# Four heads scored together in the last unit, the last batch leaving in two parts, moved fills and a reordered expert choice in a one-core attention kernel

## The chip, the cores and the metric

The kernel runs on one NeuronCore of a Trainium2 chip. A core has five engines with queues of their own: TensorE (PE; its weight loads are listed apart as PEld), VectorE (DVE), ScalarE (ACT), GpSimd (POOL), and SyncE (SP), which here only issues DMA transfers. TensorE multiplies a stationary operand with a moving one and writes to PSUM, eight banks of 512 floats per partition; the other engines bring results from there to SBUF. Each engine works its own queue in order and waits on semaphores for the others. The metric is device time in microseconds (us), as the median of several runs.

## The reference

The input is 8 sequences of 1024 tokens of 256 floats. Three residual steps follow one another:

```python
x = x + 0.5 * ffn(layernorm(x), ...)      # mixture of 8 experts, top 2, capacity 1280
x = x + attention(layernorm(x), ...)      # 16 heads of 16, causal
x = x + 0.5 * ffn(layernorm(x), ...)
```

In `ffn` each token chooses two of 8 experts by a softmax gate. An expert is kept only if at most 1280 of the 16384 choices name it:

```python
counts = jnp.bincount(a_e, length=E)
keep = counts <= cap
```

An expert that is over capacity contributes nothing. Attention is ordinary: projections to q, k, v, scores with a causal mask, softmax, values, an output projection with bias.

## The kernel before

The kernel bets that no expert is kept. It runs attention on `x` directly, computes the gate of both expert layers beside it and counts the choices; at the end one flag decides whether the expert layers must be run at all (`tc.If(flag(either, "either") > 0)`). With the inputs used here the branch is not taken, so the time is that of `attention` and the flag.

**Units.** `attention` (L663) works in 32 units: 8 batches of 4 groups, each of 4 heads. A head's 16 dimensions take a stripe of 32 partitions, so a group fills 128. For a unit u two series of 24 steps exist. `m_steps(u + 1)` computes the next unit's scores once for their row maxima (tiles `sm`; VectorE reduces them into `first` and `top`). `e_steps(u)` computes this unit's scores again, transposed and with the maximum subtracted (tiles `sc`, 128 keys by up to 512 queries); ScalarE takes the exponential into `pT`, POOL zeroes the masked part of blocks on the diagonal (`affine_select`), and TensorE multiplies with the values (`pav`). A unit has two halves `hf` of 512 queries, with 4 and 8 blocks `jb` of 128 keys; a step k is one pair `pr` of heads of one block. The step loop issues the two scores of one pair, each followed by one of the next unit's maxima: four matmuls on four stripes of rows. Value products are owed for two or three steps and then issued in two parts. In the last unit (u = 31) there is no next unit, and a step has only its own two scores.

**PSUM.** Six single-bank buffers rotate over all score tiles (`score`), and two (`bank`) over everything else: value sums, projections, transposes.

**Order.** While attention runs, `InOrder` (L27) keeps each compute engine's instructions in the order of the program text. Its line, L37, therefore stands for nearly all instructions in the profile. `Beside` (L52) mixes side work into the steps: a generator yields a number of steps to wait, or `PIECE`, and a call of `step` then runs one piece. `settle` (L871) transposes the maxima and makes `qE`, the query with its maximum; `project` (L801) makes q and k of two groups and sends each head's rows to its stripe by DMA (`kT`, `qT`); `values_of` makes the values.

**Leaving.** The value sums of a group are copied to SBUF (`att`) and stored to DRAM (`att_d`). After the fourth group of a batch, `leave(b, hf)` (L954) loads all 16 heads and their softmax sums back in another layout (`on`, `sums`), inverts the sums, sends them through DRAM to spread them (`inv_d`, `inv`), multiplies on POOL, and projects (`px`, eight 32-column matmuls per block of 128 tokens), adding to the residual `xa`. `ln_stats` and `regate` (L1004) then give the second gate's logits, `choose` (L327) picks two experts per token and the tally is updated. For the last batch the first half's leave starts in step 9 of the last unit, and the second half's runs after all units:

```python
            drain(leave(B - 1, 1))
            drain(regate(B - 1, HT, TB))
```

**Choice.** `choose` subtracts the maximum logit, takes the exponential on ScalarE, normalises, and finds the largest key and then the second largest, each as a one-hot tile.

**End.** `any_kept` (L389) sums a tally over partitions with a matmul by ones, compares with the capacity and reduces to one number per layer; both numbers are combined, cast to an integer and read by all engines.

**Opening.** Weights are loaded on ScalarE's and SP's queues, transposed, and copied. VectorE first scales `bqT`, then takes the statistics of the first batch, then reduces `row16` to `one16`, a column with 1 in each stripe's 17th row. ScalarE copies `one16` into `kT` of four units (two before the first weight copy). Both halves of the first two groups are projected (L1072); of each, SP sends kT, and ScalarE's queue sends the first group's qT.

The pool tag `packed` has four buffers, used by the weights at first and by the projections after them.

Of the kernel before, what the change touches and what calls it, by code (L numbers as in the profile page):

```python
# [10 lines left out]
F32 = mybir.dt.float32  # L11
I32 = mybir.dt.int32
# [6 lines left out]
P = 128  # L19
# [81 lines left out]
def macaron_kernel(  # L101
# [59 lines left out]
    def mm(name):  # L161
# [13 lines left out]
    iota_e = const.tile([P, E], F32, name="iota_e")  # L175
    gpsimd.iota(iota_e, pattern=[[1, E]], base=0, channel_multiplier=0, allow_small_or_imprecise_dtypes=True)

    row16 = const.tile([P, 4], F32, name="row16")
    gpsimd.memset(row16, 0.0)
    gpsimd.affine_select(  # L180
        out=row16, in_=row16, pattern=[[-32, 4]], compare_op=ALU.not_equal, fill=1.0, base=-HD, channel_multiplier=1
    )
    one16 = const.tile([P, 1], F32, name="one16")
    vector.tensor_reduce(one16, row16, AX.X, ALU.max)

    tops = []
    for k in range(2):
# [20 lines left out]
    def weights(pool, bank, matmul, transpose):  # L208
# [16 lines left out]
            nc.sync.dma_start(out=boT, in_=bo.rearrange("(c p) -> p c", p=P))  # L225
            nc.sync.dma_start(out=bvT, in_=bkv[D:].rearrange("(c p) -> p c", p=P))

        vector.tensor_scalar(bqT, bqT, QSCALE, None, ALU.mult)

        def turn(wsb, dst):  # L230
            pt = bank("pt_w")
# [95 lines left out]
    def choose(rp, tag, n, lg):  # L327
        def new(name, shape=(P, n, E), dt=F32):
            return rp.tile(list(shape), dt, tag=f"{name}{n}", name=f"{name}_{tag}")

        def over_e(a):
            return a.unsqueeze(2).to_broadcast([P, n, E])

        mx = new("mx", (P, n))
        vector.tensor_reduce(mx, lg, AX.X, ALU.max)
        lc = new("lc")
        vector.tensor_tensor(lc, lg, over_e(mx), ALU.subtract)
        prob = new("prob")
        scalar.activation(prob, lc, AF.Exp)
        yield 1  # L340
        sm = new("sm", (P, n))
        vector.tensor_reduce(sm, prob, AX.X, ALU.add)
        vector.reciprocal(sm, sm)
        vector.tensor_tensor(prob, prob, over_e(sm), ALU.mult)
        yield 1

        key = new("key")
        vector.tensor_scalar(key, prob, TINY, 1.0, ALU.is_ge, ALU.subtract)
        vector.scalar_tensor_tensor(key, key, 1e30, lc, ALU.mult, ALU.min)
        yield 1  # L350
        ohs = []
        for k in range(2):
            best = new("best", (P, n))
            vector.tensor_reduce(best, key, AX.X, ALU.max)
            cand = new("cand")
            vector.tensor_tensor(cand, key, over_e(best), ALU.is_equal)
            yield 1

            vector.scalar_tensor_tensor(
                cand, cand, -100.0, iota_e.unsqueeze(1).to_broadcast([P, n, E]), ALU.mult, ALU.add  # L360
            )
            first = new("first", (P, n))
            vector.tensor_reduce(first, cand, AX.X, ALU.min)
            yield 1
            oh = new(f"oh{k}")
            vector.tensor_tensor(oh, cand, over_e(first), ALU.is_equal)
            if k == 0:
                vector.scalar_tensor_tensor(key, oh, -1e32, key, ALU.mult, ALU.add)
            ohs.append(oh)
            yield 1  # L370
        both = new("both")
        vector.tensor_tensor(both, ohs[0], ohs[1], ALU.add)
        return prob, ohs, both

    def run(steps):
        while True:
# [9 lines left out]
        return tally  # L386


    def any_kept(layer, tally, ps):  # L389
        nc.tensor.matmul(  # L390
            ps[:, : TB * E], lhsT=ones, rhs=tally.rearrange("p t e -> p (t e)"), start=True, stop=True
        )
        counts = route.tile([P, E], F32, tag="counts", name=f"counts{layer}")
        vector.tensor_reduce(counts, ps[:, : TB * E].rearrange("p (t e) -> p e t", e=E), AX.X, ALU.add)
        vector.tensor_scalar(counts, counts, float(CAP), None, ALU.is_le)
        some = route.tile([P, 1], F32, tag=f"some{layer}", name=f"some{layer}")
        vector.tensor_reduce(some, counts, AX.X, ALU.max)
        return some

    def flag(some, what):  # L400
        word = route.tile([P, 1], I32, tag="word", name=f"word_{what}")
        vector.tensor_copy(word, some)
        return nc.values_load(word[0:1, 0:1], min_val=0, max_val=1)


    def routing(layer, logits, wts, slots, idx):
        with tc.tile_pool(name=f"rt{layer}", bufs=1) as rp:
# [4 lines left out]
            def over_t(a):  # L412
                return a.unsqueeze(1).to_broadcast([P, NT, E])

            prob, ohs, both = run(choose(rp, f"r{layer}", NT, logits))

            before = new("before", (P, P))
            make_upper_triangular(nc, before, val=1.0, diag=False)
# [244 lines left out]
    def attention(run_no, src, dst, gate0, logits, tally):  # L663
# [3 lines left out]
        with stack:  # L667
# [125 lines left out]
            def gate_first(b):  # L793
                if gate0 is not None:
                    lg = gate0[0][:, b * TB : (b + 1) * TB, :]
                    both = (yield from choose(ap_route, f"f{b}", TB, lg))[2]
                    vector.tensor_tensor(gate0[1], gate0[1], both, ALU.add)

            def project(u, apart, parts=(0, 512)):  # L801
# [3 lines left out]
                for s0 in parts:  # L805
                    others = []
                    for wT, bT, dsts, scale in ((wkT, bkT, kTs, 1.0), (wqT, bqT, qTs, QSCALE)):
# [14 lines left out]
                        for k in range(8):  # L822
                            r = 32 * (k % 4)
                            to = dsts[(u + k // 4) % 4][r : r + HD, s0 : s0 + 512]
                            head = packed[HD * k : HD * (k + 1), :]
                            if apart:
                                nc.sync.dma_start(out=to, in_=head)
                            elif k < 4:
                                (nc.sync if dsts is kTs else scalar).dma_start(out=to, in_=head)
                            else:  # L830
                                others.append((to, head))
                        if apart:
# [48 lines left out]
            def e_steps(u):  # L881
# [28 lines left out]
                def values(hf, jb, pTs, part):  # L910
# [10 lines left out]
                    for pr in (1, 0):  # L921
                        for h in range(2):
# [6 lines left out]
                                start=(jb == 0 and part == 0),  # L929
                                stop=(jb == 4 * hf + 3),  # L930
                            )
                    if jb == 4 * hf + 3 and part == 0:
                        att = ap.tile([P, 512], F32, tag="att", name=f"att{u}_{hf}", bufs=4)
                        scalar.copy(att, pav.pop(hf))
                        if g == 0:
                            att_ds[b, hf] = spill.tile(
                                [NH, 32, 512], F32, tag="att_d", name=f"att_d{run_no}_{b}_{hf}", bufs=3
                            )
                        nc.sync.dma_start(
                            out=att_ds[b, hf][4 * g : 4 * g + 4].rearrange("h r c -> (h r) c"), in_=att  # L940
                        )
# [59 lines left out]
                )  # L1001


            def regate(b, j0, j1):  # L1004
                xb = xbs[b]
                n = j1 - j0
                while light:
                    light.popleft()()
                rstd = ln_rstd(gate_lns[b][1][:, j0:j1, :], f"g{b}_{j0}")
                yield 3  # L1010
                lg = logits[:, b * TB + j0 : b * TB + j1, :]
                vector.tensor_tensor(
                    lg, xb[:, j0:j1, D:], rstd[:, :n].unsqueeze(2).to_broadcast([P, n, E]), ALU.mult
                )
                both = (yield from choose(ap_route, f"g{b}_{j0}", n, lg))[2]
                vector.tensor_tensor(tally[:, j0:j1], tally[:, j0:j1], both, ALU.add)

            def drain(steps):
                for _ in steps:
# [54 lines left out]
                scalar.copy(kT, one16.to_broadcast([P, S]))  # L1074
            beside = Beside()
            opening = beside.add(chain(some(turning, 2), values_of(0, 0, 0, HT)))
            owed, light = deque(), deque()
            STEPS = 24

            long_steps = [*range(4), *range(8, 20)]  # L1080
            for u in range(-1, NU):
# [25 lines left out]
                for k in range(0, STEPS, 2) if u < 0 else ():  # L1107
# [4 lines left out]
                    if k == 8:  # L1112
                        beside.add(settle(0, 0), first=True)
                    beside.step(True)
                for k in range(STEPS) if u >= 0 else ():


                    scores, then = es[k]
# [10 lines left out]
                        then(part)  # L1129
                    if light:  # L1130
                        light.popleft()()
                    if g == 3 and u >= 0 and k == 9:

                        beside.add(chain(leave(b, 0), regate(b, 0, HT) if b + 1 == B else ()))
                    if g == 0 and b and k == 2:
                        beside.add(chain(leave(b - 1, 1), regate(b - 1, 0, TB)))
                    if g == 1 and k == 7 and b + 1 < B:
# [8 lines left out]
                        settling = beside.add(settle(u, 1), first=True)  # L1146
                    if k == 7 and u >= 0:
                        beside.finish(settling)
                    beside.step(k in long_steps or u in (0, NU - 1) or beside.pending() > 1)
            while owed:  # L1150
                _, then, part = owed.popleft()
                then(part)
            while beside.works:
                beside.finish(beside.works[0])
            drain(leave(B - 1, 1))
            drain(regate(B - 1, HT, TB))
            for e in (pe, vector, scalar, gpsimd):
                e.keep = False


    logits = [route.tile([P, NT, E], F32, name=f"logits{k}") for k in range(2)]
    tallies = [tally_tile("0"), tally_tile("1")]
    attention(0, x, out, (logits[0], tallies[0]), logits[1], tallies[1])

    def kept_at_all(layer, tally):
        with ExitStack() as stack:
            ffn_banks(stack, f"count{layer}")
            return any_kept(layer, tally, acc(f"cnt{layer}"))

    somes = [kept_at_all(f"{k}", tallies[k]) for k in range(2)]  # L1170
    either = route.tile([P, 1], F32, name="either")
    vector.tensor_tensor(either, somes[0], somes[1], ALU.max)
    with tc.If(flag(either, "either") > 0):

        with tc.If(flag(somes[0], "0") > 0):
            feed_forward(0, logits[0], x, xw_d)
            tally = tally_tile("1b")
            attention(1, xw_d, out, None, logits[1], tally)
            vector.tensor_copy(somes[1], kept_at_all("1b", tally))
        with tc.If(flag(somes[1], "1") > 0):  # L1180
            feed_forward(1, logits[1], out, out)


# [38 lines left out]
```

## Time and profile before

| | us |
|---|---|
| median of 3 runs (1480.86 to 1483.59) | 1483.27 |
| profiled execution, its own time | 1481.55 |
| span of that execution | 1479.8 |
| TensorE busy | 1411.9 |
| VectorE busy | 1061.8 |
| ScalarE busy | 789.9 |
| POOL busy | 397.1 |
| first score matmul of the last unit starts | 1400.39 |
| its last value product ends | 1430.74 |
| last instruction of a compute engine ends | 1470.47 |

The span runs from the first to the last instruction of the profiled execution. In a list of instructions a line has the start, the duration, the engine, the operation, output and inputs by the program's names, shapes and how many were merged (x8). A float32 matmul appears as two records, one for each pass. In a list of stretches each stretch of the span has its length and then, for PE, PEld, DVE, ACT and POOL, the busy time with the number of instructions, then the granted TensorE clock, the DMA engines' share and GB/s. In the chain of work each line has start, duration, and the work, DMA, queue or engine that released the next.

### The profile page before, as it was taken

To read this page: it belongs to the slowest core of one execution; us is meant where nothing else is said; L and a number is where in the kernel's file an instruction comes from. 1 tells how busy PE (TensorE), PEld (TensorE's weight loads), DVE (VectorE), ACT (ScalarE), POOL (GpSimd) and SP (SyncE) were. 2 spreads that over 40 slices of the span, in tenths; PEclk is the share of its full clock that TensorE was granted. 3 is DMA by queue.
4 is the path that set the end of the run, shared out by engine and by line. 5 is a ranking of instruction groups with operands and counts; after the bars stand their busy time and mean duration, and the time that the engine had idled before them with its cause. 6 is when DMAs were issued, how large, how long until landed. Compare 5 with 4: busy or idle time off the path is not lost.

```text
span 1479.8 us, 38173 instructions
## 1 busy us (share of the span) xinstructions
PE 1411.9 (95%) x14760; PEld 554.8 (37%) x14760; DVE 1061.8 (72%) x3395; ACT 789.9 (53%) x1790; POOL 397.1 (27%) x713
## 2 busy tenths in 40 slices
PE   5999999999999999999999999999999999999972
PEld 2434333343434333343333334343333434334320
DVE  2857678777877767777787777877677777778622
ACT  2255555555555565555555555555655556555640
POOL 2015114241143313142141411433131421321121
PEclk9999999999999999999999999999999999999995
DMA  4010111211021210212112111212112111121010
GB/s 138 9 37 23 37 33 43 67 58 47 29 62 55 69 37 32 64 41 80 31 46 66 58 45 30 64 49 72 37 32 62 42 51 31 47 66 37 23 61 32
DMA packets 58224, 71.93 MB, mean 49 GB/s; under 512 B 15912, under 2 KB 33456, under 8 KB 58032
## 3 DMA queue, kind: packets, MB, share of 16 engines
q1 hardware_dynamic: 56688, 68.60, 15.6%
q8 instruction: 118, 1.93, 0.5%
q10 hardware_dynamic: 1344, 0.79, 0.2%
q14 instruction: 74, 0.61, 0.1%
HBM read 26.88 MB, written 25.69 MB: 36 GB/s over the span
## 4 chain that ended last, share of the span: by engine, by line
PE 86%; DVE 6%; POOL 2%; ACT 2%; DMA 2%; issue 1%; SPq 0%; ACTq 0%; DVEq 0%; POOLq 0%
PE sc L37 39%; PE pav L37 20%; PE pq L37 8%; PE sm L37 7%; PE pv L37 4%; PE px L37 4%; DVE sm L37 2%; PE pm L37 2%; DVE qE L37 2%; PE pta L37 1%; ACT pT L37 1%; DMA att_d<-att 1%; POOL rstd_a L37 1%; POOL xa L37 1%; POOL pT L37 1%
## 5 line engine op out<-in xcount | busy, mean ns | idle before, releaser
L37 ACT ACTIVATE pT<-sc 128x512 f32<-128x512 f32 (+3 forms) x1536 | 669.3, 488 | 550.0 <-PE sm L37 448.0
L37 PE MATMUL sm<-kT,qT 32*128 32x512 f32 (+3 forms) x3072 | 786.1, 536 | 1.7 <-DVE top L37 0.5
L37 PE MATMUL sc<-qE,kT 32*128 32x512 f32 (+3 forms) x3072 | 736.6, 534 | 1.3 <-ACT pT L37 1.3
L37 POOL TENSOR_SCALAR_AFFINE_SELECT pT<-pT 128x256 f32<-128x256 f32 x512 | 207.1, 407 | 987.7 <-ACT pT L37 984.4
L37 DVE TENSOR_REDUCE first<-sm 128x1 f32<-128x512 f32 x512 | 328.7, 684 | 150.2 <-PE sm L37 147.2
L37 PE MATMUL pav<-pT,vaug 128*32 128x256 f32 (+2 forms) x5120 | 386.7, 371 | 1.7 <-POOL pT L37 1.7
L37 PEld LDWEIGHTS sc<-qE,kT 32*128 32x128 f32 x3072 | 261.4, 183 | 336.8 <-ACT pT L37 237.4
L37 DVE CUSTOM_DVE_ANT_0 sm<-sm,causal,first 128x256 f32<-128x256 f32 (+3 forms) x512 | 262.1, 555 | 94.2 <-PE sm L37 86.0
L37 PEld LDWEIGHTS sm<-kT,qT 32*128 32x128 f32 x3072 | 299.3, 184 | 23.6 <-DVE top L37 11.8
L37 DVE CUSTOM_DVE_ANT_0 sm<-sm,causal 128x256 f32<-128x256 f32 (+3 forms) x512 | 241.3, 514 | 72.0 <-PE sm L37 52.4
L37 PEld LDWEIGHTS pav<-pT,vaug 128*32 128x32 f32 x5120 | 102.7, 108 | 333.1 <-issue 221.6
L37 DVE DVE_READ_ACCUMULATOR2_ANT top<- 128x1 f32 x1024 | 144.5, 141 | 0.0
L37 PE MATMUL px<-woT,on 128*32 128x264 f32 x1024 | 81.8, 402 | 20.1 <-POOL on L37 18.2
L37 PE MATMUL pv<-wvT,xnT 128*32 128x264 f32 x1024 | 82.1, 393 | 1.7 <-DVE qE L37 1.6
L37 PE MATMUL pq<-xnT,wkT 128*32 128x512 f32 x512 | 69.7, 621 | 3.7 <-ACT xnT L37 3.7
L37 POOL TENSOR_SCALAR xn_a<-xa,mv_a,rstd_a 128x256 f32<-128x256 f32 x56 | 67.7, 1222 | 19.1 <-PE pta L37 19.0
L37 PE MATMUL pq<-xnT,wqT 128*32 128x512 f32 x512 | 66.8, 596 | 0.8 <-ACT packed L37 0.8
L37 PEld LDWEIGHTS px<-woT,on 128*32 128x32 f32 x1024 | 30.4, 112 | 55.2 <-POOL on L37 20.3
L37 DVE TENSOR_TENSOR qE<-qT,pm 128x512 f32<-128x512 f32 x64 | 43.5, 679 | 3.2 <-PE pm L37 2.3
L37 POOL TENSOR_TENSOR on<-on,inv 128x512 f32<-128x512 f32 x32 | 40.6, 1270 | 11.2 <-DMA inv<-inv_d 11.2
L37 PEld LDWEIGHTS pv<-wvT,xnT 128*32 128x32 f32 x1024 | 29.8, 110 | 36.6 <-issue 15.5
L37 POOL TENSOR_TENSOR xa<-xa,bo_all 128x528 f32<-128x528 f32 x32 | 41.8, 1307 | 2.8 <-issue 2.3
(113 smaller groups left out, 552.3 us busy)
## 6 DMA issues: line engine op xcount, KB each, us to landing
att_d<-att SPq DMA_DIRECT2D x64, 256.0 KB
kT<-packed SPq DMA_DIRECT2D x256, 32.0 KB
on<-att_d SPq DMA_DIRECT2D x32, 256.0 KB
inv<-inv_d SPq DMA_DIRECT2D x32, 256.0 KB
out_dram<-xa SPq DMA_DIRECT2D x16, 512.0 KB
qT<-packed SPq DMA_DIRECT2D x248, 32.0 KB
xa<-in_L_attn_x_dram SPq DMA_DIRECT2D x7, 1024.0 KB
xa<-in_L_attn_x_dram SPq DMA_DIRECT2D x2, 512.0 KB
```

The costliest lines, as they stand in the source:

```text
L37: i = call(*args, **kwargs)
```

## The change

- The opening: `one16` is made on POOL by a fill and four selects instead of one select and a VectorE reduction. `bqT` is scaled on POOL. ScalarE issues no transfers in `project`: SP sends kT and qT of the first group, then those of the second.
- `choose`: the first expert is found from the logits whose difference to the maximum is zero, ahead of the softmax; the second as before. The two one-hot tiles are added to the tally one after the other.
- Unit 30: from step 9 the new `leave_most` brings the first twelve heads of the last batch's first half back, as `leave` does, with `on`'s upper half of its second chunk zeroed.
- Unit 31: the loop takes two steps at once. The four heads' scores of a block are issued together, then the value products owed from the block before, then two pieces of side work. Step 0 adds `leave_most` of the second half. Step 8 adds `leave_last` of the first half: it copies the last four heads' sums to SBUF, transposes them on TensorE, normalises on VectorE, transposes back, and projects (128 rows by 264 columns) onto the residual; `regate` follows.
- After the units: the first layer's count, `leave_last` and `regate` of the second half, and the second count, which now run in attention's own banks. The flag is made from the smallest count by two instructions.

```diff
-    row16 = const.tile([P, 4], F32, name="row16")
...
-    vector.tensor_reduce(one16, row16, AX.X, ALU.max)
+    gpsimd.memset(one16, 0.0)
+    for k in range(4):
+        gpsimd.affine_select(
...
-        vector.tensor_scalar(bqT, bqT, QSCALE, None, ALU.mult)
+        gpsimd.tensor_scalar(bqT, bqT, QSCALE, None, ALU.mult)
...
+        vector.tensor_scalar(cand, lc, 0.0, -100.0, ALU.is_equal, ALU.mult)
+        lowest(ohs[0])
...
-                            if apart:
+                            if apart or k < 4:
                                 nc.sync.dma_start(out=to, in_=head)
-                            elif k < 4:
-                                (nc.sync if dsts is kTs else scalar).dma_start(out=to, in_=head)
...
+                for k in range(0, STEPS, 2) if u == NU - 1 else ():
+
+                    then = es[k + 1][1]
+                    for h in range(2):
+                        es[k][0](h)
+                        es[k + 1][0](h)
+                    owed.append((0, then, 0))
+                    owed.append((0, then, 1))
+                    while len(owed) > 2:
+                        _, then, part = owed.popleft()
+                        then(part)
+                    if k == 0:
+                        beside.add(leave_most(b, 1, (1, 3, 3, 3)))
+                    if k == 2:
+                        beside.add(settle(u, 1), first=True)
+                    if k == 8:
+                        beside.finish(most)
+                        copies = (vector.tensor_copy, vector.tensor_copy)
+                        beside.add(chain(leave_last(b, 0, last.pop(), copies), regate(b, 0, HT)), first=True)
+                    for _ in range(2):
+                        if light:
+                            light.popleft()()
+                        beside.step(True)
...
+                    if u == NU - 2 and k == 9:
+                        most = beside.add(leave_most(b, 0, (2, 3, 3, 3)))
...
-            drain(leave(B - 1, 1))
+            leasts = [None if gate0 is None else fewest("0", gate0[1], bank("cnt0"))]
+            drain(leave_last(B - 1, 1, last.pop(), (scalar.copy, vector.tensor_copy)))
             drain(regate(B - 1, HT, TB))
+            leasts.append(fewest("1" if gate0 else "1b", tally, bank("cnt1")))
```

The new function for the last four heads:

```diff
+            def leave_last(b, hf, pav, copies):
...
+                for k in range(2):
+                    copies[k](att[:, k * 256 : k * 256 + 256], pav[:, k * 256 : k * 256 + 256])
+                yield PIECE
+                pt = bank(f"pt_last{hf}")
+                for i in range(4):
+                    transpose(pt[:, i * P : (i + 1) * P], att[:, i * P : (i + 1) * P])
+                heads = pt.rearrange("p (i h r) -> p i h r", i=4, h=4)
...
+                vector.reciprocal(inv, heads[:, :, :, HD])
+                for i in range(4):
+                    vector.tensor_tensor(
+                        normed[:, i, P // 2 :].rearrange("p (h d) -> p h d", h=4),
...
+                for i in range(4):
+                    transpose(pt[:, i * P : (i + 1) * P], normed[:, i])
+                for k in range(2):
+                    copies[k](on[:, k * 256 : k * 256 + 256], pt[:, k * 256 : k * 256 + 256])
+                for i in range(4):
+                    yield PIECE
+                    j = hf * HT + i
+                    px = bank(f"px_last{hf}_{i}")
+                    matmul(px[:, : D + E], on[:, i * P : (i + 1) * P], woT[:, 1, :])
+                    vector.tensor_tensor(xb[:, j, :], px[:, : D + E], xb[:, j, :], ALU.add)
+                    ln_stats(xb, j, *gate_lns[b])
```

`leave_most` is `leave` with `late = 12` heads instead of 16, waits given as arguments, both chunks of a projection in one piece, and neither the statistics nor the store, which `leave_last` does.

## The prediction

> **What bounds the kernel now.** I read the page first (shares and the slices), then stretches of the span for each engine, then the chain of work at both ends, and last TensorE's order of time in the last two units.
>
> ```profile
> span 1479.8 us, 38173 instructions
> PE 1411.9 (95%) x14760; PEld 554.8 (37%) x14760; DVE 1061.8 (72%) x3395; ACT 789.9 (53%) x1790; POOL 397.1 (27%) x713
> ...
> 1380.00:1430.00 50.00, 49.36 (x471) 18.45 (x469) 17.27 (x46) 33.36 (x78) 9.48 (x24) 1.00 0.09 29
> 1430.00:1440.00 10.00, 4.72 (x72) 2.27 (x70) 4.94 (x15) 0.58 (x1) 3.82 (x5) 0.91 0.34 110
> 1440.00:1450.00 10.00, 0.00 (x0) 0.00 (x0) 4.42 (x22) 0.23 (x1) 0.18 (x1) 0.50 0.09 31
> 1450.00:1460.00 10.00, 6.76 (x64) 2.61 (x64) 1.57 (x4) 0.00 (x0) 2.52 (x2) 0.56 0.08 25
> ```
>
> TensorE is full (second column) until 1430 us. After that the kernel is a serial tail: from the last value product (1430.74) to the last word (1470.47) are 39.7 us; then 9.3 us without an instruction on the compute engines close the span. The tail's chain (start, us, what):
>
> ```profile
> 1430.24 2.50 POOL on L37 x2
> ...
> 1432.78 3.37 PE px L37 x56
> ...
> 1447.71 4.90 DMA inv<-inv_d
> ...
> 1454.00 5.70 PE px L37 x56
> ```
>
> Both halves of the last batch leave here, one after the other, the second through a round trip by DRAM. In the last unit, TensorE in order of time:
>
> ```profile
> 1400.39 1.14 PE L37 MATMUL sc<-qE,kT 32*128 32x512 f32 x8
> ...
> 1413.01 1.13 PE L37 MATMUL sc<-qE,kT 32*128 32x512 f32 x4
> 1414.07 0.64 PE L37 MATMUL pav<-pT,vaug 128*32 128x256 f32 x8
> 1414.64 1.13 PE L37 MATMUL sc<-qE,kT 32*128 32x512 f32 x4
> ```
>
> Four heads back to back (x8) take what two take (x4): 1.14 against 1.13. With no maxima of a next unit beside them, two scores leave half of the array's rows idle. At the other end the chain is
>
> ```profile
> 2.44 6.66 DMA bqT<-in_L_attn_bq_dram
> 9.13 0.17 DVE bqT L37
> ...
> 13.60 1.99 ACT kT L37 x2
> ...
> 16.13 1.98 PE pta L37 x8
> ```
>
> VectorE's first instruction waits for a 1 KB vector; ScalarE's fills wait for a reduction behind VectorE's statistics; the first transposes wait for the fills.
>
> **What the Trainium skill says.** *TensorEngine Tiling (Array Packing)*, "Key Properties": tiles on different rows work in parallel; the lines above agree. The same page, "PSUM Bottleneck": after a fourfold gain the copy out of PSUM may bound; an exponential of 512 columns takes 0.54 us here, four 2.16, so ScalarE's work in the last unit is about 21 us, still under TensorE's. *PSUM — Partial Sum Buffer*, "PSUM bank collisions raise a hardware error": two engines must be kept off one bank by semaphores, so I count ScalarE's and VectorE's half copies of one bank one after the other; no trace of before has such a pair. *TensorE: Matmul & The Clock Gate*, "What's actually happening": a cold array runs at half rate until some 3.4 us of work; the trace has 0.85 us for four projections at 19 us, 0.43 at 22.
>
> **The change, part by part**, against the profiled execution (span 1479.8, its own time 1481.55; the runs' median is 1483.27, so differences are carried over to the median).
>
> *Opening.* The bqT scaling moves to POOL, whose queue is filled to 8.05; three more one-column selects, at most 0.2 each, end it near 8.6, still before bqT's landing at 9.10. So that wait is kept, but on POOL: the first rstd comes at about 10.7 (9.1 + 0.2 scaling + 0.3 + 1.05 + hand-offs). VectorE may start when x has landed. SP's queue bounds that: its load of bo_all, queued behind x's first half, is issued at 5.72, bvT, behind the second, at 8.28. Statistics are then done by about 10.4, and the xn at 10.8 instead of 13.49. ScalarE's fills, now behind POOL's selects (about 5.2), and both weight copies end by 9.7. Transposes start at 11.15 instead of 16.13, the first projection at 13.8 instead of 18.77: 5.0 gained.
> Second half: ScalarE no longer issues four qT loads (2.53 us at 24.71) ahead of xnT. But SP now issues kT, qT of unit 0, then kT, qT of unit 1, 16 x 0.63 = 10.1 us, from 18.0 to 28.1. The pool gives packed's third and fourth tile the first two's buffers: they wait for kT_1's and qT_1's transfers, landing (1.4 us from issue, as inv_d<-sums: 1445.62 to 1447.07) at about 27 and 29. So packed ends near 30 instead of 34.5, and the transposes queued behind it on TensorE (wvT, for the first values) stand at 30.3 instead of 34.80. Then ScalarE's fills (2.0) and wvT (0.7): 33 instead of 39.55. Unit 0's later score maxima need qT's second half, issued by 33 and landed by 35; they come at 36. Gain 4.5 (by TensorE's transposes) to 6.5 (by wvT): **-6.0**. If the landings take 3 us, -4; if the array is warm sooner, -7.5. Were x later than SP's queue says, VectorE would start at 9.13 as now, and the xn, then behind statistics, rstd and 13.2 us, would give back 2.5.
>
> *Choice.* 20 VectorE instructions per choice before, 20 after (`both` goes, one product and one tally addition come); only the exponential's 0.3 us wait is covered. In units 0 to 30 TensorE bounds and its order is unchanged: **0** (from -2 to +2, as VectorE is 70 to 80% busy and its order does change).
>
> *Unit 30* gets the first twelve heads' leave: two POOL multiplications (1.26 each) between selects with 0.4 to 0.9 us of idle before them. The sums need att_d (issued 1378.56, 2 to 3.3 to landing) and 2 more; the reciprocal stands at about 1385.5: no stall. **0**; uncovered, up to +2.
>
> *Unit 31.* TensorE's work: scores 3.00 + 7.28 (four heads of 512, 384, 256, 128 columns take 1.07, 0.86, 0.64, 0.43 in unit 30) = 10.3; values 0.35 + 2.98 + 7.54 = 10.9; eight twelve-head projections of 2 x 0.58 = 9.3; four last-head ones of 0.58 = 2.3; settling and two rounds of transposes 1.8; a count 0.3: **34.9**. Waits: px_1 for a bank that att's copy frees only behind four exponentials, 1.25; px_2 for qE in the other bank, 0.8; the transposes for VectorE's copies and normalisation (0.35 + 0.2 + four of 0.21), 1.05; four times a second projection of a pair for the addition that frees its bank, 0.57 each = 2.3; the last selection 1.0. Together 6.4, so 41.5 instead of 30.35 (1400.39 to 1430.74): **+11.1**. ScalarE (21) and VectorE (16) hide below. Waits that the change adds there: VectorE's reciprocal of the second half's sums stands between px_2's and px_3's additions, about 10 us into the unit; att is stored at 4.4, landed by 7.7 (3.3 as at 1366.87 to 1370.18), the sums by 9.8 (2.1 as at 1414.86 to 1417.0). Were it late, px_3's bank and the next scores would be late by as much. POOL's two multiplications for the second half wait for inv (reciprocal 10.5, inv_d 1.4, inv 4.0 and 5.1 as in the tail's chain: 17 to 18 us into the unit); queued behind them are the rstd and the selects of the last diagonal, wanted at 29, so 10 us of slack, and nothing unless inv takes three times as long. On SP the last batch's transfers stand alone.
>
> *Tail.* Copies 0.8; transposes, reciprocal, four products, transposes 0.25 + 0.25 + 0.9 + 0.25; a copy 0.45; first projection 0.6; four times addition, statistics, aggregate (0.43 + 0.42 + 0.18) 4.1; rstd 1.5; regate, 21 instructions of 0.22, 4.7; count 0.75; two reductions and the flag 0.65: 15.2 instead of 39.7: **-24.5**. The stores overlap the regate. The closing 9.3 stay.
>
> Sum: -6.0 + 11.1 - 24.5 = -19.4. Span 1460.4, profiled time 1462.1; median 1483.27 - 19.4 = **1463.9**.
>
> **Rivals.**
> A, the above, 1464 (own range 1459 to 1469): 0.58.
> B, the last unit runs faster than unit 30: px ran at 0.45 per chunk in the tail (spacing 0.89 of the additions) against 0.58 in dense stages. If the waits let TensorE keep that pace, 34.9 shrinks by up to a fifth, 6 us: 1458. For it: the idle share; against: unit 31 before, with half the rows idle, kept the slow pace. 0.14.
> C, the opening gives nothing, as SP's 16 serial issues and the buffer waits put packed where it was: 1470. For: everything but issue times is inferred; against: issues end at 28.1, not 34. 0.16.
> D, the four heads do not run together: two of them wait for banks that ScalarE frees (six banks, four needed), up to 0.5 for each of eight large steps: 1468. Against: ScalarE is done with a step before TensorE returns. 0.05.
> E, slower: the granted clock. It averages 0.980, with stretches of 0.72 to 0.84 before 120 us. 0.01 of it is 14 us of TensorE's 1412; from 0.966 down the gain is gone (1484 and more). Against: three runs lie within 0.2%. 0.04.
> The remaining 0.03 are mixtures.
>
> **How the numbers follow.** The likeliest is A. 1456 to 1472 takes in A, nearly all of C and D, and B's middle. About 0.2% is what a measurement of this kernel can tell from no change: within it lies only a failed tail with C (0.02); faster 0.94; slower 0.04.
>
> **What would show it.** Opening: first transposes near 11, packed's third copy near 27 waiting for transfers, SP busy with packed's transfers from 18 to 28. Unit 31: four scores of 512 in 1.07, about 41 us from first score to last value, TensorE waits of 0.5 to 1.3 ahead of px_1, px_2 and each second projection. Tail: 15 us from last value to the flag, no DRAM round trip in the chain. Wrong if POOL or VectorE stand on the chain within unit 31, if unit 31 exceeds 46, or if units 1 to 29 differ from before.

## The result, and the profile after

The changed kernel takes **1504.65 us** (median of 4 runs, 1501.92 to 1506.36) against 1483.43 (4 runs, 1480.86 to 1484.96) of the kernel before on the same chip: a ratio of 1.0143, 95% interval 1.0122 to 1.0164. It is 21 us slower, where 19.4 us less were forecast. Its profiled execution took 1506.36 us with a span of 1504.6.

First the parts that the prediction had worked out. On the page, the span and the busy shares of the changed kernel:

```profile
span 1504.6 us, 38256 instructions
PE 1439.3 (96%) x14792; PEld 564.8 (38%) x14792; DVE 1083.3 (72%) x3415; ACT 789.7 (52%) x1790; POOL 400.8 (27%) x721
```

TensorE is busy 27 us longer for 32 more matmuls, VectorE 21.5 us longer for 20 more instructions. Neither was to be expected from the counts.

The opening's chain of work in the changed kernel:

```profile
2.43 6.32 DMA bqT<-in_L_attn_bq_dram
8.83 0.26 POOL bqT L37
...
11.11 1.96 PE pta L37 x8
...
28.75 1.99 DMA qT<-packed
...
31.58 1.12 PE pt_w L37 x4
```

The first transposes stand at 11.11 (11.15 was predicted, 16.13 before), the transposes for the values at 31.58 (30.3 predicted, 34.80 before).

The last unit's order of time on TensorE, with idle time before an instruction and what ended it in brackets:

```profile
1438.47 1.15 PE L37 MATMUL sc<-qE,kT 32*128 32x512 f32 x8
...
1442.28 1.10 PE L37 MATMUL px<-woT,on 128*32 128x264 f32 x16 [1.42 <-ACT att L37]
...
1446.60 1.10 PE L37 MATMUL px<-woT,on 128*32 128x264 f32 x16 [0.78 <-DVE qE L37]
```

The stretches of the tail (columns as before: length, then PE, PEld, DVE, ACT, POOL, the clock, DMA share, GB/s):

```profile
1470.00:1480.00 10.00, 8.20 (x108) 3.51 (x96) 5.21 (x24) 5.09 (x16) 3.39 (x9) 1.00 0.00 1
1480.00:1490.00 10.00, 4.80 (x15) 2.68 (x14) 5.65 (x22) 0.37 (x1) 1.27 (x2) 0.74 0.16 55
1490.00:1500.00 10.00, 0.69 (x2) 0.50 (x2) 3.79 (x22) 0.23 (x1) 0.00 (x0) 0.50 0.04 8
```

From the first score of unit 31 (1438.47) to its last value product (1479.11) are 40.64 us, from there to the last compute instruction (1495.19) 16.1, and 9.4 close the span. So from unit 31 on the kernel is 13.2 us shorter than before (66.2 against 79.4), and yet unit 31 starts 38.1 us later. The loss lies in between, where TensorE's order is the same in both kernels.

**Where it gathers.** A unit's length is taken here from the start of its first exponential (`pT<-sc`, 48 in each unit) to that of the next unit:

| units | before | after |
|---|---|---|
| 4, 8, ... 28 (b from 1 to 7, first group) | 44.48 to 44.95 | 47.29 to 50.51, mean 49.51 |
| 6, 10, ... 26 (third group) | 44.43 to 44.51 | 44.94 to 45.16 |
| 5, 9, ... 21 and 7, 11, ... 27 | the same within 0.2 | the same within 0.2 |
| 25 and 29 | 42.99 and 41.46 | 43.41 and 42.51 |
| 2 to 30 together | 1244.3 | 1283.1 |

In units 4b the loss sits between steps 6 and 9. Unit 4 is shown. VectorE, in order of time:

```profile
251.71 0.27 DVE L37 TENSOR_SCALAR cand_f<-cand_f 128x64 f32<-128x64 f32 x1
252.01 1.23 DVE L37 TENSOR_TENSOR cand_f<-cand_f,iota_e 128x64 f32<-128x64 f32 x1
253.28 0.22 DVE L37 TENSOR_REDUCE first_f<-cand_f 128x8 f32<-128x64 f32 x1
253.53 0.23 DVE L37 TENSOR_TENSOR oh_f<-cand_f,first_f 128x64 f32<-128x64 f32 x1
253.67 0.29 DVE L37 CUSTOM_DVE_ANT_0 sm<-sm,causal 128x128 f32<-128x128 f32 x1
253.88 0.14 DVE L37 DVE_READ_ACCUMULATOR2_ANT top<- 128x1 f32 x1
...
254.13 1.47 DVE L37 TENSOR_TENSOR tally<-tally,oh_f 128x64 f32<-128x64 f32 x2
```

POOL at the same time:

```profile
251.89 1.27 POOL L37 TENSOR_TENSOR on<-on,inv 128x512 f32<-128x512 f32 x1
253.12 0.91 POOL L37 TENSOR_SCALAR_AFFINE_SELECT pT<-pT 128x256 f32<-128x256 f32 x2
253.99 1.27 POOL L37 TENSOR_TENSOR on<-on,inv 128x512 f32<-128x512 f32 x1
```

An addition of 64 columns, 0.22 us elsewhere, takes 1.23. It begins 0.12 after POOL's multiplication for the leave of the batch before and ends 0.08 after it; the first tally addition ends 0.08 after the second multiplication. The maxima `sm` queued behind on VectorE are late by as much, and TensorE waits for their bank:

```profile
252.62 0.27 PE L37 MATMUL sc<-qE,kT 32*128 32x128 f32 x1
254.08 0.48 PE L37 MATMUL sm<-kT,qT 32*128 32x128 f32 x2 [1.19 <-DVE top L37]
...
255.92 1.98 PE L37 MATMUL sm<-kT,qT 32*128 32x512 f32 x2
```

The two passes of a 512-column score take 1.15 at full clock; the last line has 1.98. The stretches of the changed kernel show why:

```profile
250.00:252.50 2.50, 2.50 (x37) 1.27 (x35) 2.43 (x12) 1.08 (x4) 0.98 (x2) 1.00 0.22 53
252.50:256.00 3.50, 2.31 (x23) 1.04 (x23) 3.40 (x13) 0.47 (x3) 2.73 (x4) 1.00 0.32 84
256.00:259.50 3.50, 3.50 (x13) 0.53 (x10) 1.50 (x4) 1.08 (x2) 0.00 (x0) 0.51 0.00 0
259.50:263.00 3.50, 3.50 (x28) 1.11 (x24) 1.15 (x2) 1.14 (x3) 0.00 (x0) 0.52 0.00 0
```

In the kernel before, the first and the third of these stretches are:

```profile
250.00:252.50 2.50, 2.50 (x37) 1.29 (x40) 2.37 (x13) 0.88 (x5) 0.74 (x2) 1.00 0.24 54
256.00:259.50 3.50, 3.50 (x36) 1.00 (x32) 2.23 (x6) 2.27 (x5) 0.00 (x0) 1.00 0.03 9
```

After 1.19 us of idle time the granted clock (third column from the right) falls to half for 6.8 us, though TensorE is busy without a break (13 and 28 matmuls in the last two stretches; 36 in each of them in the kernel before). Between 120 us and unit 31 the trace of before has no half-clock stretch. That of after has six, in units 4, 8, 12, 16, 20 and 28, together 37.5 us, of which half, 18.8, is lost. The rest of the 33.5 us of these seven units, 14.7, is the waiting and what it brings, 2.1 per unit; unit 24, which has the wait and no drop, lost 2.34. The gap is at most 1.19 of that. For the rest the late maxima ran by themselves and not beside the scores of their step: in unit 24 two records of `sm` with 128 columns alone for 0.48 us right after the gap, and two with 512 columns from 1149.29 to 1150.41, for the most part alone.

In units 4b + 2 the second gate's choice puts four instructions ahead of `qE`, and the value projection behind it waits 0.75 us instead of 0.27.

### The profile page after: what moved, and what is told of

Read it like the earlier page. It is cut to its first block, busy times and chain, and to the rows that moved or that the text cites. A ratio compares the mean times of both kernels' runs of the same rounds, so it can differ in the third digit from the quotient of the medians.

```text
span 1504.6 us, 38256 instructions
## 1 busy us (share of the span) xinstructions
PE 1439.3 (96%) x14792; PEld 564.8 (38%) x14792; DVE 1083.3 (72%) x3415; ACT 789.7 (52%) x1790; POOL 400.8 (27%) x721
## 4 chain that ended last, share of the span: by engine, by line
PE 83%; DVE 8%; POOL 2%; DMA 2%; ACT 2%; issue 1%; SPq 0%; ACTq 0%; DVEq 0%; POOLq 0%
PE sc L37 38%; PE pav L37 19%; PE pq L37 8%; PE sm L37 7%; PE pv L37 4%; PE px L37 4%; DVE sm L37 3%; DVE qE L37 2%; PE pm L37 2%; PE pta L37 1%; ACT pT L37 1%; DMA att_d<-att 1%; POOL rstd_a L37 1%; DVE cand_f L37 1%; DMA kT<-packed 1%
## 5 line engine op out<-in xcount | busy, mean ns | idle before, releaser
L37 PE MATMUL sm<-kT,qT 32*128 32x512 f32 (+3 forms) x3072 | 807.6, 543 | 9.7 <-DVE top L37 8.0
L37 PEld LDWEIGHTS sm<-kT,qT 32*128 32x128 f32 x3072 | 306.1, 186 | 37.4 <-DVE top L37 23.7
L37 PE MATMUL pq<-xnT,wqT 128*32 128x512 f32 x512 | 72.8, 646 | 0.8 <-ACT packed L37 0.8
L37 PE MATMUL pm<-ident,top 128*128 128x128 f32 x256 | 42.0, 287 | 0.0
```

The costliest lines, as they stand in the source:

```text
L37: i = call(*args, **kwargs)
```

## The experiments

Each was measured with the kernel before on the same chip (its medians 1480.72 to 1480.98 there).

**The choice undone, and the choice alone.** In the first kernel `choose` and its callers are those of before, all else is the change; the second is the reverse.

```diff
-        vector.tensor_scalar(cand, lc, 0.0, -100.0, ALU.is_equal, ALU.mult)
-        lowest(ohs[0])
...
+        both = new("both")
+        vector.tensor_tensor(both, ohs[0], ohs[1], ALU.add)
```

> The changed kernel with the choice of before (20 instructions spread over nine steps, one addition to the tally); opening, units 30 and 31 and the tail stay changed. Theory P (the reordered choice puts two plain VectorE additions behind POOL's two 1.27 us multiplications in each unit 4b, TensorE then waits 1.2 us for a score bank and its clock falls to half): all of the 39 us that gather between units 4 and 31 go, 1504.65 - 39 = about 1466, no TensorE gap over 0.6 us between 120 us and unit 31, no half-clock window there. Theory K (the clock falls by itself, from power or phase, whatever the choice): the half-clock windows stay, at most half comes back, above 1480. Theory U (unit 30 and the last unit, not the choice): stays near 1504.

> The kernel before with the reordered choice and its two tally additions, and nothing else of the change. Theory P: the same 39 us come on top of before, 1483.4 + 39 = about 1522, with a gap of about 1.2 us on TensorE in units 4, 8, ... 28. Theories K and U: within 5 us of before.

Choice undone: 1465.97 (1464.88 to 1467.53), ratio 0.9906 (0.989 to 0.9923). Units 2 to 30 take 1244.3, as before to the tenth; there is no half-clock stretch between 120 us and unit 31, and TensorE's waits for `top` are gone. Choice alone: 1521.36 (1515.63 to 1521.84), ratio 1.0264 (1.0239 to 1.0288), units 2 to 30 1282.8 with the same six drops. The choice is the whole loss, 38.5 to 38.8 us in these units, and the half clock follows from it.

**The burst, or the moment.** All bursts stay, only their place in units 4b moves.

```diff
-                    beside.add(gate_first(b))
+                    beside.add(chain((12,), gate_first(b)))
```

> The changed kernel; only the first gate's choice starts 12 steps later in units 4b, among blocks of 512 columns, where POOL has no multiplication. All bursts of four and five VectorE instructions remain. Theory P: 33.5 us (the excess of the seven units 4b) come back, about 1471 to 1474; cand + iota and the tally additions of the first gate take 0.22 us instead of 0.67. Theory B (it is the bursts themselves, not the shared moment with POOL): they cost as much at the new place, above 1495.

1463.09 (1458.58 to 1465.11), ratio 0.9881 (0.9855 to 0.9907), better than expected. Units 4b take 43.62 to 43.81 and lose nothing to the bursts. VectorE's groups of this kernel (count, busy time, mean ns):

```profile
L37 DVE TENSOR_TENSOR tally<-tally,oh_f 128x64 f32<-128x64 f32 x16 | 3.8, 237 | 0.3
L37 DVE TENSOR_TENSOR cand_f<-cand_f,iota_e 128x64 f32<-128x64 f32 x16 | 3.6, 225 | 0.6
```

The same groups of the changed kernel, with the same instructions beside POOL's multiplications:

```profile
L37 DVE TENSOR_TENSOR tally<-tally,oh_f 128x64 f32<-128x64 f32 x16 | 10.7, 670 | 0.3
L37 DVE TENSOR_TENSOR cand_f<-cand_f,iota_e 128x64 f32<-128x64 f32 x16 | 10.7, 667 | 0.5
```

**Which instructions wait.** The first of these two fuses the factor and the addition of iota into one instruction; the second keeps the count and writes the plain forms with a scalar of 1.0.

```diff
-            vector.tensor_tensor(cand, cand, iota_e.unsqueeze(1).to_broadcast([P, n, E]), ALU.add)
+            vector.scalar_tensor_tensor(
+                cand, cand, -100.0, iota_e.unsqueeze(1).to_broadcast([P, n, E]), ALU.mult, ALU.add
+            )
...
-        vector.tensor_scalar(cand, cand, -100.0, None, ALU.mult)
```

> The changed kernel with the factor -100 and the addition of iota in one VectorE instruction with scalar and two tensors, as before had it; places and bursts stay, one instruction fewer per choice. Theory P with the block by POOL tied to two operands in SBUF: the fused instruction has two as well and also waits (about 1.2 us), the time stays at 1500 to 1505. Theory P with the block tied to the plain two-tensor form: it takes 0.3 us, TensorE's 1.2 us gap goes, the tally addition still waits but alone; about 1475 to 1485.

```diff
-            vector.tensor_tensor(oh, cand, over_e(first), ALU.is_equal)
+            vector.scalar_tensor_tensor(oh, cand, 1.0, over_e(first), ALU.mult, ALU.is_equal)
...
-                        vector.tensor_tensor(gate0[1], gate0[1], oh, ALU.add)
+                        vector.scalar_tensor_tensor(gate0[1], gate0[1], 1.0, oh, ALU.mult, ALU.add)
```

> The changed kernel with the additions of iota, the comparisons with the lowest and the first gate's tally additions written as instructions with a scalar (1.0) and two tensors: same places, same number, same operands. If any two operands in SBUF wait for POOL's multiplication: they take 1.2 us as the plain form does, units 4b take 48 to 50.5 us, the time stays near 1504. If only the plain two-tensor form waits: about 0.3 us each, units 4b about 44.7 us, about 1468 to 1471 (the 0.7 us per unit 4b + 2 stay).

Fused: 1490.16 (1487.35 to 1490.58), ratio 1.0067 (1.005 to 1.0084), between both expectations and for neither's reason. In unit 4 of its trace POOL's multiplication runs from 250.91 to 252.18:

```profile
250.74 0.29 DVE L37 SCALAR_TENSOR_TENSOR cand_f<-cand_f,iota_e 128x64 f32<-128x64 f32 x1
251.06 0.22 DVE L37 TENSOR_REDUCE first_f<-cand_f 128x8 f32<-128x64 f32 x1
251.31 0.95 DVE L37 TENSOR_TENSOR oh_f<-cand_f,first_f 128x64 f32<-128x64 f32 x1
```

With one instruction less the addition came 0.17 before POOL's and was through; the reduction, with one tensor operand, was not held back; the comparison, the next with two, waited for the rest. TensorE's gap shrank to 0.67 us and one drop of the clock was left. With all forms changed: 1505.53 (1501.88 to 1509.11), ratio 1.016 (1.0124 to 1.0196), units 2 to 30 1282.9:

```profile
L37 DVE SCALAR_TENSOR_TENSOR tally<-tally,oh_f 128x64 f32<-128x64 f32 x16 | 10.7, 670 | 0.3
L37 DVE SCALAR_TENSOR_TENSOR cand_f<-cand_f,iota_e 128x64 f32<-128x64 f32 x16 | 10.7, 667 | 0.5
```

The form does not matter. The two tensor operands in SBUF do.

**Which POOL instruction holds them.** POOL multiplies by a constant, so that it reads one tensor. This leaves out the division by the softmax sums; the second gate then keeps an expert and the expert layers are run, so the total, 2070.92 (2068.57 to 2072.7), says nothing and only the units count.

```diff
-                    gpsimd.tensor_tensor(on[:, c], on[:, c], inv[:, c], ALU.mult)
+                    gpsimd.tensor_scalar(on[:, c], on[:, c], 1.0, None, ALU.mult)
```

> The changed kernel; POOL multiplies on by 1.0 instead of by inv in the leave of batches 0 to 6 (both halves), so that it reads one SBUF tensor; the division by the softmax sums is left out there. If a POOL instruction with one SBUF operand holds VectorE's second operand back as well: cand + iota and the tally additions take as much as POOL's instruction has left, time near 1500. If only POOL's two-operand instruction does: they take 0.3 to 0.5 us, as behind POOL's normalisation in the trace of before, units 4b about 45 us, 1470 to 1476.

Units 4b take 45.47, units 2 to 30 1254.9, and the clock does not drop. Here POOL's instruction runs from 251.03 to 252.61, longer than the multiplication:

```profile
251.02 0.23 DVE L37 TENSOR_TENSOR cand_f<-cand_f,iota_e 128x64 f32<-128x64 f32 x1
251.28 0.22 DVE L37 TENSOR_REDUCE first_f<-cand_f 128x8 f32<-128x64 f32 x1
251.54 0.26 DVE L37 TENSOR_TENSOR oh_f<-cand_f,first_f 128x64 f32<-128x64 f32 x1
```

The comparison begins with 1.07 left of it and takes 0.26. Where the addition of iota stood with 1.15 us of the multiplication left, it now starts 0.01 ahead of POOL, so the comparison is the only witness: half a microsecond after its start this POOL instruction does not hold VectorE back, where the multiplication did (0.95 for the same comparison above).

That it reads only one tensor does not explain this. POOL's selects on `pT` read one tensor too, and they do hold VectorE. In the kernel before, in unit 6:

```profile
335.22 0.41 POOL L37 TENSOR_SCALAR_AFFINE_SELECT pT<-pT 128x256 f32<-128x256 f32 x1 [1.45 <-ACT pT L37]
335.26 0.44 DVE L37 TENSOR_TENSOR oh_g<-cand_g,first_g 128x64 f32<-128x64 f32 x1
```

The comparison had 0.36 of the select left, and ended 0.08 after it. POOL's scaling of `xn_a` by two values per row (1.22 us, one tensor) holds VectorE only for a first part: in the changed kernel a tally addition that began at 134.34 with 1.06 us of it left was done when 0.59 were left. Whether the scaling by a constant holds VectorE in its first half microsecond as well is not shown, since no two-operand instruction began there.

**Lateness alone.** The kernel before with two reductions (one operand, results unused) in units 4b, after step 5 or after step 13.

```diff
+                    if g == 0 and u > 0 and k == 5:
+                        for _ in range(2):
+                            spare = ap.tile([P, 1], F32, tag="spare", name=f"spare{u}")
+                            vector.tensor_reduce(spare, woT, AX.XY, ALU.max)
```

> The kernel before with two more VectorE reductions (one SBUF operand of 528 floats, about 0.65 us each, results unused) after step 5 of units 4, 8, ... 28, just ahead of the maxima of the 128-column blocks: VectorE is late by 1.3 us without any two-operand instruction behind POOL. Theory P: VectorE's lateness is what counts: a TensorE gap of about 1 us, then half clock, as in the changed kernel, 3 to 5 us per unit, +20 to +35 us, about 1503 to 1518. Theory L (the lock itself slows more than VectorE): under +5.

> The same two reductions after step 13 of the same units, among blocks of 512 columns, where VectorE idles about 0.6 to 0.9 us in each 2.2 us. Theory P with the place deciding: TensorE has two banks' worth of slack and the lateness is caught up in two steps, 0 to +0.7 us per unit, no half clock, 1483 to 1488. If the place does not matter: as the run with the reductions after step 5.

After step 5: 1504.12 (1499.22 to 1504.81), ratio 1.0165 (1.0144 to 1.0186). In its trace 1.30 us of reductions stand ahead of the 128-column maxima, and TensorE's next maxima wait:

```profile
250.20 1.30 DVE L37 TENSOR_REDUCE spare<-woT 128x1 f32<-128x528 f32 x2
```

```profile
251.82 0.48 PE L37 MATMUL sm<-kT,qT 32*128 32x128 f32 x2 [0.92 <-DVE top L37]
```

Units 4b take 46.44 to 49.85, three of the seven with a half-clock stretch. After step 13 the same 1.3 us cost nothing: 1480.76 (1477.5 to 1482.84), ratio 0.9998 (0.9985 to 1.001), units 2 to 30 1244.3. So VectorE's lateness is enough, without a two-operand instruction behind POOL ahead of that gap, and it is the place that makes it dear: blocks of 128 columns, where VectorE has hardly any idle time. (A little later in the first run the next two-operand instruction, moved back by the reductions, met POOL's multiplication too; part of its +23 us is that.)

**Opening and last units, each alone.** The kernel before with only these parts of the change.

```diff
-        vector.tensor_scalar(bqT, bqT, QSCALE, None, ALU.mult)
+        gpsimd.tensor_scalar(bqT, bqT, QSCALE, None, ALU.mult)
...
-                            if apart:
+                            if apart or k < 4:
```

> The kernel before with the changed opening alone (bqT and the column of ones on POOL, qT sent by SP). The recorded step says -6.0 (from -4 to -7.5). The changed kernel's trace shows -3.2 at the first score of unit 0 and -0.9 at unit 4, a half-clock window of 6.8 us at 58 us having taken the rest. If that window is tied to the new opening: -1, 1482.5. If it is chance from run to run: -3, 1480.5.

```diff
+                    if u == NU - 2 and k == 9:
+                        most = beside.add(leave_most(b, 0, (2, 3, 3, 3)))
...
-            drain(leave(B - 1, 1))
+            drain(leave_last(B - 1, 1, last.pop(), (scalar.copy, vector.tensor_copy)))
```

> The kernel before with the changed units 30 and 31 and the changed tail alone (choice and opening of before). The recorded steps say +11.1 - 24.5 = -13.4; the changed kernel's trace shows +10.3 - 23.0 = -12.7. About 1470.5. Were unit 30 hurt by the first twelve heads' leave, above 1473.

Opening: 1475.72 (11 runs, 1472.27 to 1477.95), ratio 0.9966 (0.9954 to 0.9979), that is 5.0 us less (3.1 to 6.8); both of my readings from one trace were too low. Before 120 us every trace has half-clock stretches, 13.7 to 34.1 us in all, and kernels with the same opening differ in them (17.1, 23.9, 34.1), so one execution cannot tell a gain of this size. Last units: 1467.69 (1464.13 to 1468.17), ratio 0.9911 (0.9888 to 0.9933), 13.2 us less (9.9 to 16.6).

The three parts add up: 39.1 - 5.0 - 13.2 = +20.9 us, against 21.2 measured for the whole.

**The kernel before pays as well.** Only the later start of the first gate's choice, then a version with all that helped: opening, units 30 and 31 and tail of the change, the choice of before, 12 steps later, and the copy of unit 30's last value sums on VectorE.

```diff
-                        scalar.copy(att, pav.pop(hf))
+                        (vector.tensor_copy if (u, hf) == (NU - 2, 1) else scalar.copy)(att, pav.pop(hf))
```

> The kernel before with one edit: the first gate's choice starts 12 steps later in units 4b. Theory P: -7.3 us (seven units of 43.62 instead of 44.67), about 1473.6. If the gain there belongs to the reordered choice: within 1 us of before.

> Opening, units 30 and 31 and the tail as changed; the choice of before; the first gate's choice 12 steps later in units 4b; and the copy of the last value sums of unit 30 on VectorE instead of ScalarE. Theory P says that the choice of before pays for POOL's multiplications too (one instruction of 0.62 us): units 4b took 43.62 us with the later choice against 44.67 in the kernel before, 7 x 1.05 = 7.3 less than the run with the choice of before; the copy takes up to 1.2 us of the 1.42 us wait at the head of unit 31. About 1458 (1480.98 - 23). If the later choice helps only the reordered one: about 1465.

The later start alone: 1476.43 (19 runs, 1471.47 to 1479.53), ratio 0.9971 (0.9961 to 0.9981), 4.3 us less; units 4b take 44.10 to 44.38, not the 43.62 that I had carried over from the reordered choice. The traces show where the rest goes: the choice of before runs over more steps, so that its last two additions now stand ahead of the 128-column maxima at the end of the unit, and TensorE waits 0.31 us there for `top` in each of the seven units; up to that wait unit 4 keeps step with that of the run with the later reordered choice, and behind it, it is 0.48 late. All together: 1461.52 (1461.37 to 1461.99), ratio 0.987 (0.9843 to 0.9896), 19 us under the kernel before and, by the two ratios (0.987 / 1.0143), some 40 under the changed one. The 1.42 us wait at the head of unit 31 is gone:

```profile
1396.55 2.14 PE L37 MATMUL px<-woT,on 128*32 128x264 f32 x32
```

Its units 2 to 30 take 1240.7. The reordered choice for the first gate (43.62) with that of before for the second (44.43) was not tried.

## Why the prediction was wrong

**Choice, "0 (from -2 to +2)": this step failed, by 39 us.** It compared numbers of instructions and let each keep its duration. The order was known: `choose` of the first gate had moved so that additions with two SBUF operands stood at steps 5 and 6 of units 4b, beside POOL's multiplications of steps 5 and 7. The profile of before had the sign of it. There the same kind of instruction met the same multiplication, at a cheaper moment; its groups (busy time, mean ns of one):

```profile
L37 DVE TENSOR_TENSOR cand_f<-key_f,best_f 128x64 f32<-128x64 f32 x16 | 6.8, 422 | 0.6
...
L37 DVE TENSOR_TENSOR cand_g<-key_g,best_g 128x64 f32<-128x64 f32 x14 | 3.2, 225 | 0.5
```

Equal shape and operation, 422 against 225: seven of the sixteen lasted 0.62 to 0.99 us, each until POOL's multiplication was done. Asking why would have shown the rule, and the Trainium skill states it: *SBUF — State Buffer*, "Who interferes with whom": a VectorE instruction with two SBUF inputs contends with a GpSimd instruction that reads SBUF, over ports that only one of them can have. The runs agree for POOL's multiplication (1.23 us with 1.15 left, whatever VectorE's form; one-operand reductions untouched) and for its selects (0.44 with 0.36 left); POOL's scaling by a constant, which reads SBUF too, did not hold the comparison (0.26 with 1.07 left).

"In units 0 to 30 TensorE bounds and its order is unchanged" was the second half of the error. TensorE bounds them with so little slack in the blocks of 128 columns that VectorE, 1.0 us late, makes it wait 1.19. The step's remark that VectorE is 70 to 80% busy is a mean; in the stretch from 250 to 252.5, in these blocks, VectorE of the kernel before was busy 2.37 of 2.50 (shown above).

**Rival E** gave the granted clock as a way to be slower, at 0.04, and came nearest, but in part only. The mean went from 0.980 to 0.973, which by the rival's own rate of 14 us for 0.01 is 10 us; the half clock in units 4b cost 18.8, and the other half of the 39 us is not clock at all. The rival gave no cause for a fall of the clock. The cause was in the change: the gaps that it made. The prediction took what the Trainium skill says of a cold array into the opening only, and no gap in the middle was looked for.

**The rest held,** the opening partly by luck. Opening -6.0 (from -4 to -7.5): -5.0 measured. But the transposes for the values stand only 3.2 us earlier (forecast 4.5), and so does the first score of unit 0 (57.93 against 61.09; 57.2 to 58.6 in the eight traces with the new opening, 60.3 to 61.7 in the six with the old). In the trace of the opening alone, the rest goes with the clock, which was at half for 3.4 us between that score and 120 us against 10.2 in the kernel before; the prediction has no term for that. First transposes within 0.04 us, packed's fourth copy done at 31.5 instead of near 30, as SP's sixteen issues ended at 29.3 and not 28.1; rival C is out. Unit 30: 37.44 against 37.69, so 0 was right. Unit 31: 40.64 against 41.5 (the terms given, 34.9 and 6.4, add up to 41.3), with the named waits of 1.42, 0.78, 1.32 around the transposes, 2.18 for the second projections and 0.74 for the last selections, 6.4 in sum as forecast. Tail 16.1 against 15.2, the closing 9.4. Rival B did not come (eight matmuls of a projection took 0.55, not 0.45), nor did D (the scores of four heads took 1.15). Opening and last units without the choice gave 1465.97, 15.0 under the kernel before on that chip, where 19.4 had been said for the whole.

The last sentence of the prediction named the sign that came true: units 1 to 29 differ from before.

## What to carry to other kernels

When an instruction is moved, look up what every other engine does at its new place: two-operand VectorE work on SBUF is to be kept clear of POOL's instructions that read SBUF, of long ones above all (a multiplication of 1.27 us cost up to 1.0, a select of 0.41 some 0.2), and a group whose mean duration is twice that of its like in the same profile is the sign that they meet. Count a short stall of TensorE at more than its length, since it may take the clock with it; side work belongs into stages where VectorE has idle time, not where blocks are small.

## What the runs showed of the hardware

- A gap of about a microsecond in a busy stream of matmuls can halve TensorE's clock for 3.4 or 6.8 us. In units 4b the clock fell after 15 of 18 gaps of 1.18 or 1.19 us (the changed kernel, the choice alone, all forms changed), after 3 of 3 gaps of 0.89 to 0.95 in these kernels, after 3 of 7 of 0.84 to 0.92 (reductions after step 5), after 1 of 6 of 0.67 (fused) and after none of 7 of 0.15 to 0.21 (POOL with one operand). *TensorE: Matmul & The Clock Gate*, "What's actually happening" lists the cold state after an idle window of some 3.4 us; here a third of that was enough.
- The 18 gaps lie in the same units of three kernels and are not 18 independent cases: the three without a drop are all in unit 24. The traces show why. In each, all changes of the clock lie on a grid of 3.413 us (within 0.003), and an edge of it cuts just these three gaps near the middle (in the changed kernel 1146.27 to 1147.45, the edge at 1146.93), so that at most 0.78 us stand on one side. Of the 15 with a drop each has 0.96 or more between two edges, and the clock falls at the second of these. Of the other gaps with 0.84 to 0.96 between two edges 6 of 8 were followed by a drop, of those with 0.52 to 0.78 1 of 11. So in these units the idle time within one stretch of the grid counts, and not the length of the gap. In unit 31 a gap of 1.42 us, whole between two edges in six of seven traces, was not followed by a drop in any of the traces with it; what else counts is open.
- A blocked VectorE instruction ends 0.08 us after POOL's multiplication or select, so it takes what is left of it plus 0.08.
- Between the opening and the tail the kernel repeats itself: units 2 to 30 together took 1244.3 us in five traces, though single units differ by up to 0.4: the kernel before, the choice undone, the opening alone, the last units alone, and the reductions after step 13.
